# Layer-2 attention scores as 64-row products in both row halves of the array

## The chip, the cores and the metric

The kernel runs on one core of one Trainium2 chip. The metric is the device time of one execution in microseconds (us). The engines are TensorE (PE, whose weight loads are listed apart as PEld), VectorE (DVE), ScalarE (ACT), GpSimd (POOL) and SyncE (SP, which issues most of the DMAs). Each engine works through its own instructions in a fixed order and waits for the others at semaphores.

## The reference, cut to what matters

The program is a Mamba block (layer 0) and then a position-attention block (layer 1 in the reference's count, the "second layer" here) on x of shape (4, 512, 32, 32). Only the second layer is touched by the change:

```python
x_top    = conv1x1(x, w_top,    b_top)     # (b, 64, 1024): 64 channels, hw = 1024
x_center = conv1x1(x, w_center, b_center)  # (b, 64, 1024)
x_bottom = conv3x3(x, w_bottom, b_bottom)  # (b, 512, 1024)
sp_map = einsum('bnp,bpm->bnm', x_center.T, x_top)      # p = 64: the scores, 1024 x 1024
sp_map = softmax(sp_map.reshape(b, -1), axis=1)         # over all of an image's scores at once
sp_map = einsum('bnm,bmc->bnc', sp_map, x_bottom.T)
out = conv3x3(x + sp_map.reshape(b, c, h, w), w_out, b_out)
```

The sum over p in the scores has 64 terms, half of the 128 rows of the PE array. The softmax is over a whole image, so nothing may be exponentiated before the maximum of all 1024 x 1024 scores of that image is known.

## The kernel before, in words

Layer 0 is one long planned stream and ends at about 1866 us of the profiled span. The second layer follows, image by image (b = 0 to 3), and there the order of each engine's instructions is set by the tile framework's scheduler: it moves instructions of one engine past each other where data allow it, and what it chose is then fixed.

For each image the work goes through these functions.

- `norm` (for images 1 to 3) normalises the image into the padded tile `xg`.
- `scores` computes `pt`, the top and center convolutions at once: four accumulating 128x512 products for each half h of the pixels, top channels in partitions 0 to 63 of `pt`, center channels in 64 to 127. ACT copies them to SBUF with the bias, `center` in one 64x512 instruction and `top` in four 64x128 ones, since top's columns are reordered into four row phases r and two column phases k. Both tiles hold 128 partitions: the data sit in 0 to 63, and two POOL memsets write zeros into 64 to 127. Then for each of eight blocks m of 128 top columns and each half h, one product `psc` (128 rows, half of them zeros) goes to a PSUM bank, ACT copies the bank to `st[m]`, and after both halves DVE takes the row maximum into `mx`.
- After the eighth block DVE reduces `mx` to `mp`, POOL takes the maximum over partitions (`partition_all_reduce`, tile `ma`), DVE negates it, and ACT exponentiates the eight `st` tiles with the sums into `rs`, which DVE reduces to `rp`.
- `conv3` computes the 3x3 convolution by a Winograd scheme. POOL and DVE make the row inputs `rr` (from `e`, `f`, then `g`, `h`, then `k`, `l`, in a ring of four buffers), DVE `spread`s them into `v` (four instructions, lines 1461 to 1464), and PE makes 24 products `m`, each of four accumulating 128x512 matmuls with a 1 MB weight tile `uw` that SP loads into a ring of three. The products go by pairs of row points, (1,2), (3,4), (0,5), and for each point p through q = 2, 1, 0, 3. `m[2]` is read by ACT into `e_b` (line 1588), `m[1]`, `m[0]` and `m[3]` by DVE into `n_b` (line 1596).
- `attend` multiplies the exponentiated scores with the convolution (`pat`) and adds the result to `xg`; then `conv3` runs again with the output weights (`m_o`), and `turn_back` transposes its result (`po`) and adds it to `o`.

PSUM has eight banks here: pool `pm` with a ring of five for the `m` products, and pool `ps` with a ring of three for everything else (`pt`, `psc`, `pat`, `po`). A new tile can be written only when the tile that held its bank before has been read. So product (2,1) of a convolution needs the bank of (1,2), which is free after ACT's `e_b` of point 1, and (3,1) needs the bank of (2,2), free after `e_b` of point 2.

The convolution of image b and the scores of image b are independent up to `attend`, and PE runs `psc` and the first `m_b` products close together. ACT's instructions in the order before: copies of `psc`, `e_b` of point 1, the eight exponentials, `e_b` of point 2. For images 1 and 3 ACT and POOL also prepare the output convolution of the image before (`e_o`, `f_o`, then POOL's `g_o`, `h_o`) in the same stretch; the order on POOL there is `e_o`, `g_o`, `ma`, `f_o`, `h_o`.

The tiles `top` and `center` come from pool `fp`, tag `f4`, a ring of three that they share with the output tiles `o` of `finish`. For image 2 this matters: `o_3` of image 1 takes the buffer of `o_0`, `top` that of `o_1` and `center` that of `o_2`, each once its store has landed.

Of the kernel before, what the change touches and what calls it, by code (L numbers as in the profile page):

```python
# [8 lines left out]
F32 = mybir.dt.float32  # L9
AF = mybir.ActivationFunctionType  # L10
ALU = mybir.AluOpType
AX = mybir.AxisListType
# [3 lines left out]
P = 128  # L16
B, C, HH, WW = 4, 512, 32, 32
L = HH * WW
# [5 lines left out]
T = 512  # L24
NH = L // T
NB = B * NH
PAB = 64
# [4 lines left out]
    xp=(1, 2, 1),  # L32
# [184 lines left out]
def mamba_then_pab_kernel(  # L217
# [25 lines left out]
    nc = tc.nc  # L243
# [20 lines left out]
    pb_sb = cpool.tile([P, 1], F32, tag="pb", name="pb_sb")  # L264
# [58 lines left out]
    with ExitStack() as l0:  # L323
# [985 lines left out]
        for b in range(B):  # L1309
            at = b * NDC * NS  # L1310
            for n in range(NDC):
                e, h = divmod(n, NH)
# [30 lines left out]
    with ExitStack() as l1:  # L1343

        pm = l1.enter_context(tc.tile_pool(name="l1pm", bufs=5, space=PSUM))
        ps = l1.enter_context(tc.tile_pool(name="l1ps", bufs=3, space=PSUM))
        wp = l1.enter_context(tc.tile_pool(name="l1w", bufs=1))

        TI, TJ = HH // 4, WW // 2
# [6 lines left out]
        xp = l1.enter_context(tc.tile_pool(name="l1x", bufs=2))  # L1356
        fp = l1.enter_context(tc.tile_pool(name="l1f", bufs=3))

        NMC = L // P
# [40 lines left out]
        def scores(b, xg):  # L1400

            top = fp.tile([P, L], F32, tag="f4", name=f"top_{b}")
            center = fp.tile([P, L], F32, tag="f4", name=f"center_{b}")
            nc.gpsimd.memset(top[PAB:P, :], 0.0)
            nc.gpsimd.memset(center[PAB:P, :], 0.0)
            for h in range(NH):
                pt = ps.tile([P, T], F32, tag="ps", name=f"pt_{b}_{h}")
                for c in range(NCC):  # L1410
                    nc.tensor.matmul(
                        pt, wt_sb[:, c].rearrange("p j n -> p (j n)"),
                        xg[:, c, 1 + h * HR : 1 + (h + 1) * HR, 1 : WW + 1],
                        start=(c == 0), stop=(c == NCC - 1),
                    )
                nc.scalar.activation(
                    center[0:PAB, h * T : (h + 1) * T], pt[PAB:P], AF.Identity, bias=pb_sb[PAB:P]
                )
                tv = top[0:PAB].rearrange("p (r k i j) -> p r i j k", r=4, k=2, j=TJ)
                pv = pt[0:PAB].rearrange("p (i r j k) -> p r i j k", r=4, j=TJ, k=2)  # L1420
                hi = slice(h * TI // 2, (h + 1) * TI // 2)
                for r in range(4):
                    nc.scalar.activation(
                        tv[:, r, hi], pv[:, r], AF.Identity, bias=pb_sb[0:PAB]
                    )
            mx = spool.tile([P, NMC], F32, tag="mx", name=f"mx_{b}")
            st = []
            for m in range(NMC):
                t = xp.tile([P, L], F32, tag="st", name=f"st_{b}_{m}", bufs=NMC)
                for h in range(NH):  # L1430
                    pt = ps.tile([P, T], F32, tag="ps", name=f"psc_{b}_{m}_{h}")
                    nc.tensor.matmul(
                        pt, top[:, m * P : (m + 1) * P], center[:, h * T : (h + 1) * T],
                        start=True, stop=True,
                    )
                    nc.scalar.copy(t[:, h * T : (h + 1) * T], pt)
                nc.vector.reduce_max(mx[:, m : m + 1], t, axis=AX.X)
                st.append(t)
            mp = spool.tile([P, 1], F32, tag="mp", name=f"mp_{b}")
            nc.vector.reduce_max(mp, mx, axis=AX.X)  # L1440
            ma = spool.tile([P, 1], F32, tag="ma", name=f"ma_{b}")
            nc.gpsimd.partition_all_reduce(ma, mp, P, bass_isa.ReduceOp.max)
            nc.vector.tensor_scalar_mul(ma, ma, -1.0)
            rs = spool.tile([P, NMC], F32, tag="rs", name=f"rs_{b}")
            for m in range(NMC):
                nc.scalar.activation(
                    st[m], st[m], AF.Exp, bias=ma, accum_out=rs[:, m : m + 1]
                )
            rp = spool.tile([P, 1], F32, tag="rp", name=f"rp_{b}")
            nc.vector.reduce_sum(rp, rs, axis=AX.X)  # L1450
            return st, rp
# [251 lines left out]
        left = list(range(EARLY, NPC))  # L1703
        half = len(left) // 2
        st, rp = scores(0, image[0])
        for a in range(0, B, 2):
            ins = None
            for b in (a, a + 1):
                xb = conv3(f"b{b}", image[b], ub, brow[0], behind=ins)
                also = left[b * half : (b + 1) * half] if not a else []  # L1710
                after, v = iter(()), None
                if b == a:
                    after = norm(b + 1)
                    next(after)
                    next(after)
                else:
                    v = first_inputs(f"o{a}", image[a])
                ins = attend(b, image[b], st, rp, xb, after, also)
                if b == a:
                    st, rp = scores(b + 1, image[b + 1])  # L1720
            if a + 2 < B:
                after = norm(a + 2, True)
                next(after)
            y = conv3(f"o{a}", image[a], uo, brow[1], v)
            next(after, None)
            finish(a, y)
            if a + 2 == B:
                last(a + 1, image[a + 1], None)
                break
            next(after, None)  # L1730
            finish(a + 1, conv3(f"o{a + 1}", image[a + 1], uo, brow[1]))
            st, rp = scores(a + 2, image[a + 2])
# [57 lines left out]
```

## Time and profile before

| what | value |
|---|---|
| median of 3 runs | 2896.76 us (2893.47, 2896.76, 2897.07) |
| profiled execution, its own time | 2893.83 us |
| its span | 2892.0 us |
| mean granted TensorE clock over the span | 0.988 |
| DVE busy over the span | 2284.7 us (79%) |
| ACT busy over the span | 1837.3 us (64%) |
| POOL busy over the span | 2041.5 us (71%) |
| `psc`: PE busy, 128 instructions (64 products of two passes each) | 55.8 us |
| `st<-psc` copies on ACT, 64 of 586 ns median | 37.5 us |
| `mx` reductions on DVE, 32 of 1214 ns median | 38.2 us |
| `top`, `center` memsets on POOL, 8 of 0.95 us median | about 8 us |

A product of fp32 data shows in the trace as two weight loads and two matmul passes. The listed duration of a pass (592 ns for 512 columns) is its latency; passes follow each other every 0.43 us, so that 32 passes, the scores of one image, last 13.97 us. A timeline row gives the start, the length from the first start to the last end, the engine, the line, the operation, the tile written and the tiles read, how many instructions are merged, and in brackets how long the engine stood idle before and what it waited for. The "idle" of PEld between two loads has no weight: loads run ahead of the matmuls.

### The profile page before, as it was taken

The page shows a single profiled execution, that of the slowest core. Times are in us where ns is not written, and L with a number is a line of the kernel's source. Part 1 is how long each engine was busy: PE and PEld are TensorE (multiplying, and loading weights), DVE is VectorE, ACT ScalarE, POOL GpSimd, SP SyncE. Part 2 cuts the span into 40 slices and gives each one's busy share as a digit, 9 for nine tenths or more (in the row PEclk, how much of TensorE's full clock was granted, in tenths as well). Part 3 has the DMA queues.
Part 4 walks back from the last instruction along what each step waited for, and adds up shares of the span by engine and source line. Part 5 has one row for each costly group of instructions (what it writes and reads, how often), then busy time and mean ns, then how long its engine had stood idle before and what let it go on. Part 6 is the DMA issues. An engine that isn't in the chain of part 4 may idle for free.

```text
span 2892.0 us, 36189 instructions
## 1 busy us (share of the span) xinstructions
PE 2712.5 (94%) x11720; PEld 1614.8 (56%) x11720; DVE 2284.7 (79%) x2724; ACT 1837.3 (64%) x3249; POOL 2041.5 (71%) x1243
## 2 busy tenths in 40 slices
PE   6898799999999999989989999799999999999998
PEld 2455566666676566666667766544444444444444
DVE  5579999989999889989899999868776655356254
ACT  4789899999899999899999999530300003030000
POOL 6899999899998999999999999733231341223222
PEclk9999999999999999999999999999999999999999
DMA  6766655577655577645565664768789886436587
GB/s 188 204 178 196 185 165 176 160 216 243 196 170 168 163 230 227 200 145 176 161 206 175 212 195 144 186 225 259 255 275 300 317 321 241 180 138 226 174 313 261
DMA packets 406260, 603.68 MB, mean 209 GB/s; under 512 B 47192, under 2 KB 246104, under 8 KB 381496
## 3 DMA queue, kind: packets, MB, share of 16 engines
q1 hardware_dynamic: 398456, 587.11, 64.0%
q10 hardware_dynamic: 7616, 14.26, 1.4%
q8 instruction: 94, 1.54, 0.2%
q14 instruction: 94, 0.77, 0.1%
HBM read 504.27 MB, written 96.99 MB: 208 GB/s over the span
## 4 chain that ended last, share of the span: by engine, by line
PE 44%; ACT 21%; DVE 14%; POOL 9%; issue 7%; DMA 5%; SPq 0%; POOLq 0%; DVEq 0%; ACTq 0%
PE m_o L1580 11%; PE m_b L1580 8%; ACT sc L917 5%; PE y L990 4%; DVE da L957 4%; PE pat L1632 4%; ACT da L904 4%; POOL da L980 4%; PE u L943 4%; PE po L444 3%; ACT u L904 3%; PE pxm L444 2%; PE pz L444 2%; ACT L251 2%; POOL dbx L932 1%
## 5 line engine op out<-in xcount | busy, mean ns | idle before, releaser
L980 POOL TENSOR_TENSOR da<-da,cbc 128x1024 f32<-128x1024 f32 x314 | 742.3, 2370 | 33.0 <-DVE da L957 8.3
L917 ACT ACTIVATE sc<-dtxt,bt_sb 128x256 f32<-128x256 f32 x1256 | 550.6, 498 | 18.1 <-PE u L943 17.4
L932 POOL TENSOR_TENSOR dbx<-dtx,bbc 128x1024 f32<-128x1024 f32 x198 | 467.5, 2371 | 20.3 <-PE y L990 8.8
L904 ACT ACTIVATE da<-dt,a_sb 128x512 f32<-128x512 f32 x628 | 433.5, 714 | 13.6 <-PE y L990 8.8
L957 DVE TENSOR_TENSOR_SCAN da<-da,u 128x512 f32<-128x512 f32 x328 | 383.0, 1203 | 39.7 <-PE u L943 23.0
L943 PE MATMUL u<-ident,sc 128*128 128x128 f32 x2512 | 362.3, 278 | 32.8 <-DVE da L957 19.0
L943 PEld LDWEIGHTS u<-ident,sc 128*128 128x128 f32 x2512 | 291.8, 142 | 160.5 <-issue 48.5
L957 DVE TENSOR_TENSOR_SCAN da<-da,carry_sb,u 128x512 f32<-128x512 f32 x300 | 367.3, 1261 | 14.3 <-PE u L943 10.9
L990 PE MATMUL y<-ident,da 128*128 128x128 f32 x2512 | 338.4, 276 | 29.3 <-POOL da L980 28.5
L1580 PE MATMUL m_o<-uw_o,v_o 128*128 128x512 f32 x768 | 335.7, 596 | 7.4 <-DMA uw_o<-u_o 7.4
L990 PEld LDWEIGHTS y<-ident,da 128*128 128x128 f32 x2512 | 288.7, 142 | 93.7 <-POOL da L980 54.7
L1580 PE MATMUL m_b<-uw_b,v_b 128*128 128x512 f32 x768 | 333.8, 593 | 6.2 <-ACT e_b L1588 2.9
L904 ACT ACTIVATE u<-dt,a_sb 128x512 f32<-128x512 f32 x396 | 262.4, 680 | 10.9 <-DVE da L957 6.4
L444 PE MATMUL pxm<-xt,winc 128*128 128x345 f32 (+3 forms) x704 | 243.0, 488 | 19.0 <-DVE xs L706 4.7
L1580 PEld LDWEIGHTS m_b<-uw_b,v_b 128*128 128x128 f32 x768 | 144.8, 190 | 191.6 <-issue 180.3
L1580 PEld LDWEIGHTS m_o<-uw_o,v_o 128*128 128x128 f32 x768 | 144.9, 191 | 189.8 <-issue 178.4
L444 PE MATMUL pz<-xt,winc 128*128 128x512 f32 x512 | 239.5, 599 | 1.4 <-ACT dtxt L881 1.0
L990 PE MATMUL y<-ident,dbx 128*128 128x128 f32 x1584 | 220.0, 276 | 12.7 <-DVE dbx L973 7.1
L980 POOL TENSOR_TENSOR dbx<-dbx,cbc 128x1024 f32<-128x1024 f32 x91 | 215.4, 2367 | 15.2 <-DVE dbx L957 6.9
L1632 PE MATMUL pat<-y_b,st 128*128 128x512 f32 x512 | 221.6, 593 | 1.5 <-DVE rz L1641 1.4
L990 PEld LDWEIGHTS y<-ident,dbx 128*128 128x128 f32 x1584 | 182.6, 141 | 49.3 <-issue 22.7
L1588 ACT ACTIVATE e_o<-m_o 128x512 f32<-128x512 f32 x24 | 14.3, 597 | 276.2 <-PE m_o L1580 261.8
(226 smaller groups left out, 4242.2 us busy)
## 6 DMA issues: line engine op xcount, KB each, us to landing
cbc<-bcd SPq DMA_DIRECT2D x512, 256.0 KB, 3.6
uw_b<-u_b SPq DMA_DIRECT2D x96, 1024.0 KB, 4.8
uw_o<-u_o SPq DMA_DIRECT2D x96, 1024.0 KB, 4.8
bbc<-bcd SPq DMA_DIRECT2D x198, 256.0 KB, 4.0
u_b<-work SPq DMA_DIRECT2D x192, 128.0 KB, 2.6
winc<-in_w_in_dram SPq DMA_DIRECT2D x72, 256.0 KB, 3.7
szd<-sz SPq DMA_DIRECT2D x32, 512.0 KB, 4.3
szl<-szd SPq DMA_DIRECT2D x32, 512.0 KB, 5.1
```

Source lines behind the costliest of these rows:

```text
L251: nc.scalar.preload_act_table_set("natural_log_exp_and_others")
L444: lambda k=k, lhs=lhs, rhs=rhs: nc.tensor.matmul(p()[:, at : at + cols], lhs(), rhs(), start=(k == 0), stop=(k == n - 1)),
L904: nc.scalar.activation(t, dt()[:, j], AF.Exp, scale=a_sb[:, at : at + 1])
L917: nc.scalar.activation(sc()[:, k], dtxt()[:, k], AF.Copy, scale=bt[:, at, s : s + 1])
L932: lambda: nc.gpsimd.tensor_mul(hc(), dtx(), b_bc().to_broadcast([P, 2, T])),
L943: nc.tensor.transpose(u()[:, k * P : (k + 1) * P], sc()[:, k, j, :], ident)
L957: nc.vector.tensor_tensor_scan(ht, *((hc()[:, j], u()) if on_act else (u(), hc()[:, j])), carry_sb[:, j, s : s + 1] if h else 0.0, ALU.mul ...
L980: nc.gpsimd.tensor_mul(hc(), hc(), c_bc().to_broadcast([P, 2, T]))
L990: nc.tensor.matmul(y[j]()[:, k, :], hc()[:, j, k * P : (k + 1) * P], ident, start=(s == 0 and k == 0), stop=(s == NS - 1 and k == NK - 1), ...
L1580: nc.tensor.matmul(m[q], v[:, q, k, c, :], w[:, c, :], start=(c == 0), stop=(c == NCC - 1 and not extra),)
L1588: nc.scalar.activation(e, m[2], AF.Copy, scale=al / 2)
L1632: nc.tensor.matmul(pt, st[m][:, 2 * P * j + h : 2 * P * (j + 1) : 2], xb[m // 2][:, m % 2, :], start=(m == 0), stop=(m == NMC - 1),)
```

## The change

The score products contract over 64 rows instead of 128. `top` and `center` no longer have zero rows: partitions 0 to 63 and 64 to 127 both hold data. `center` is written twice, to the lower half by ACT as before and to the upper half by DVE (`tensor_scalar_add`, straight from the same PSUM partitions). `top` is split by column phase k: even blocks m = 2r lie in partitions 0 to 63 and odd ones in 64 to 127, so ACT writes it in two instructions of 64x256 for each half where there were four of 64x128. The eight memsets are gone. The eight blocks are taken by pairs: for each half h, the even block's product is issued from the lower 64 rows into a bank of pool `ps`, then the odd block's from the upper 64 rows into a bank of pool `pm`. The copies to `st` and the maxima are as many as before, in pairs.

```diff
             center = fp.tile([P, L], F32, tag="f4", name=f"center_{b}")
-            nc.gpsimd.memset(top[PAB:P, :], 0.0)
-            nc.gpsimd.memset(center[PAB:P, :], 0.0)
             for h in range(NH):
...
                 nc.scalar.activation(
                     center[0:PAB, h * T : (h + 1) * T], pt[PAB:P], AF.Identity, bias=pb_sb[PAB:P]
                 )
-                tv = top[0:PAB].rearrange("p (r k i j) -> p r i j k", r=4, k=2, j=TJ)
-                pv = pt[0:PAB].rearrange("p (i r j k) -> p r i j k", r=4, j=TJ, k=2)
+                nc.vector.tensor_scalar_add(
+                    center[PAB:P, h * T : (h + 1) * T], pt[PAB:P], pb_sb[PAB:P]
+                )
+                pv = pt[0:PAB].rearrange("p (i r j k) -> p k r i j", r=4, j=TJ, k=2)
                 hi = slice(h * TI // 2, (h + 1) * TI // 2)
-                for r in range(4):
+                for k in range(2):
+                    tv = top[k * PAB : (k + 1) * PAB].rearrange(
+                        "p (r k i j) -> p k r i j", r=4, k=2, j=TJ
+                    )
                     nc.scalar.activation(
-                        tv[:, r, hi], pv[:, r], AF.Identity, bias=pb_sb[0:PAB]
+                        tv[:, k, :, hi], pv[:, k], AF.Identity, bias=pb_sb[0:PAB]
                     )
...
-            for m in range(NMC):
-                t = xp.tile([P, L], F32, tag="st", name=f"st_{b}_{m}", bufs=NMC)
+            for g in range(0, NMC, 2):
+                two = [
+                    xp.tile([P, L], F32, tag="st", name=f"st_{b}_{g + k}", bufs=NMC) for k in range(2)
+                ]
                 for h in range(NH):
-                    pt = ps.tile([P, T], F32, tag="ps", name=f"psc_{b}_{m}_{h}")
-                    nc.tensor.matmul(
-                        pt, top[:, m * P : (m + 1) * P], center[:, h * T : (h + 1) * T],
-                        start=True, stop=True,
-                    )
-                    nc.scalar.copy(t[:, h * T : (h + 1) * T], pt)
-                nc.vector.reduce_max(mx[:, m : m + 1], t, axis=AX.X)
-                st.append(t)
+                    pts = [
+                        pool.tile([P, T], F32, tag=tag, name=f"psc_{b}_{g}_{h}_{tag}")
+                        for pool, tag in ((ps, "ps"), (pm, "m"))
+                    ]
+                    for k, pt in enumerate(pts):
+                        rows = slice(k * PAB, (k + 1) * PAB)
+                        nc.tensor.matmul(
+                            pt, top[rows, (g + k) * P : (g + k + 1) * P],
+                            center[rows, h * T : (h + 1) * T], start=True, stop=True,
+                        )
+                    for t, pt in zip(two, pts):
+                        nc.scalar.copy(t[:, h * T : (h + 1) * T], pt)
+                for k, t in enumerate(two):
+                    nc.vector.reduce_max(mx[:, g + k : g + k + 1], t, axis=AX.X)
+                st.extend(two)
```

The built program of the changed kernel gives the order that the scheduler now chooses in the second layer; layer 0 has the same order as before. What moves:

- DVE, image 0: the upper `center` of half 0 comes before the two `rr_b` of pair (1,2), that of half 1 after them and before the four `v_b`. In the `n_b` of point 1, `rp` moves ahead of the last one.
- DVE, images 1 and 3: the upper `center` of half 0 comes after the first of the four `v_b` (1461), that of half 1 after all four. `rr_b`, `v_b` and `mx` follow, interleaved slightly differently; `mp` comes again after the second `rr_b` of pair (0,5).
- DVE, image 2: `o_3`, then the upper `center` of half 0, two `rr_b`, the upper `center` of half 1, the maxima. All `n_b` of point 1 now stand behind `rp`, and ACT's `e_b` of point 1 behind the exponentials.
- POOL, images 1 and 3: `e_o`, `f_o`, `g_o`, then `ma`; before, `f_o` stood behind `ma`.
- PE: all 16 `psc` follow `pt` directly and stand ahead of the first `m_b`. Before, two matmuls of (1,2) stood ahead of them for images 1 and 3, and all of (1,2) and (1,1) for image 2. The first product of the upper half in each half h of the pixels waits for DVE.
- SP, image 2: the load of `o_3` comes before the fourth weight load instead of after it.

## The prediction

> **What bounds the kernel now.** I read the page's busy rows first, then the groups of PE from 1860 us on (the second layer), then the waits and the timelines around the scores of each image. The busy rows and three PE groups:
>
> ```profile
> span 2892.0 us, 36189 instructions
> PE 2712.5 (94%) x11720; PEld 1614.8 (56%) x11720; DVE 2284.7 (79%) x2724; ACT 1837.3 (64%) x3249; POOL 2041.5 (71%) x1243
> ...
> L1580 PE MATMUL m_b<-uw_b,v_b 128*128 128x512 f32 x768 | 333.8, 593 | 6.2 <-ACT e_b L1588 2.9 <-DVE y_b L1620 1.6 <-DMA uw_b<-u_b 0.9
> ...
> L1432 PE MATMUL psc<-center,top 128*128 128x512 f32 x128 | 55.8, 593 | 1.3 <-POOL f_b L1481 1.3
> ```
>
> PE hardly rests in the second layer, so a microsecond of PE time there is a microsecond of the end unless another chain takes over. The m_b row names such a chain: PE already waits 2.9 us for ACT's e_b. The scores are 4 x 13.97 us of PE. Their surroundings decide what a saving is worth, so I take the images one by one. Image 1, by engine (PE, DVE, POOL, ACT in turn):
>
> ```profile
> 2047.14 13.90 PE L1432 MATMUL psc<-center,top 128*128 128x512 f32 x32
> 2067.16 24.30 PE L1580 MATMUL m_b<-uw_b,v_b 128*128 128x512 f32 x56
> 2093.56 32.02 PE L1580 MATMUL m_b<-uw_b,v_b 128*128 128x512 f32 x74 [2.10 <-ACT e_b L1588]
> ...
> 2044.04 1.23 DVE L1461 TENSOR_TENSOR v_b<-rr_b 128x1024 f32<-128x1024 f32 x1
> 2045.18 3.56 DVE L1462 TENSOR_TENSOR v_b<-rr_b 128x1024 f32<-128x1024 f32 x1
> 2048.66 3.58 DVE L1463 TENSOR_TENSOR v_b<-rr_b 128x1024 f32<-128x1024 f32 x1
> 2052.15 1.25 DVE L1464 TENSOR_TENSOR v_b<-rr_b 128x1024 f32<-128x1024 f32 x1
> ...
> 2070.97 3.27 POOL L1481 TENSOR_TENSOR e_o<-e_o,xg 128x1088 f32<-128x1088 f32 x1 [19.83 <-ACT e_o L1480]
> 2074.21 2.52 POOL L1543 TENSOR_TENSOR g_o<-xg 128x1088 f32<-128x1088 f32 x1
> 2083.20 0.38 POOL L1442 PARTITION_ALL_REDUCE ma<-mp  x1 [6.48 <-issue]
> 2090.80 2.29 POOL L1481 TENSOR_TENSOR f_o<-f_o,xg 128x1088 f32<-128x1088 f32 x1 [7.22 <-ACT st L1446]
> ...
> 2092.93 1.05 ACT L1588 ACTIVATE e_b<-m_b 128x512 f32<-128x512 f32 x2
> ```
>
> The end of this stretch is not set by PE: POOL does e_o and g_o, then spends 6.48 us before the reduction, ACT exponentiates, and only then reads the bank that PE's product (3,1) needs. PE stands 2.10 us, and 0.85 us at the same place in image 3 (a wait ending at 2600.81). DVE has no hole from 2040 to 2074.
>
> **The products.** Sixteen products take 13.97/16 = 0.87 us each. No row has two products in different row halves, so the price of a pair lies between one product (0.87) and two (1.74). I take 0.87: the two passes of a product use other rows than those of the next. ACT's two e_b above show its rate, 1.05 us for two or about 0.5 a copy; 16 copies need some 8 us and fall little behind. So 16 products would take 7 us, if nothing stands in between. [...]
>
> **What stands in between: DVE's upper center.** The first odd product of half 1 needs DVE's second copy, and PE's order lets nothing pass it. No row shows a 64x512 copy from PSUM on DVE; the nearest is n_b (128x512, one PSUM operand), 0.68 us alone and 0.60 in a row. Bounds 0.3 (half the elements) to 0.7; I take 0.6.
>
> *Image 0.* The two rr_b in front of it run 1881.04 to 1885.85, so the copy ends at about 1886.5, while PE would have had its first pair done by 1882.9. From 1886.6 on, seven slots of 0.87 remain: PE leaves the scores at 1892.7, where before it left at 1895.2. PE has stood 3.7 us by then, and what follows a stand shows in the stretches just before (columns: PE, PEld, DVE, ACT, POOL busy, then the granted clock):
>
> ```profile
> 1867.00:1871.00 4.00, 1.20 (x6) 0.59 (x4) 2.88 (x10) 0.47 (x2) 3.25 (x7) 1.00 0.78 205
> 1871.00:1873.40 2.40, 2.39 (x3) 0.80 (x4) 2.40 (x3) 0.00 (x0) 0.84 (x1) 0.59 1.04 423
> 1873.40:1876.00 2.60, 2.60 (x6) 1.17 (x5) 0.44 (x1) 2.08 (x2) 2.03 (x1) 0.72 1.00 422
> ```
>
> After 4 us with 1.2 of work the clock was 0.59, then 0.72: 2.4 x 0.41 + 2.6 x 0.28 = 1.7 us lost. So PE leaves at 1892.7 to 1894.4. [...]
>
> Then banks: product (2,0), at 1916.9 before, needs the bank of (1,1), read by DVE's n_b. DVE before: mp 1904.37, ma 1909.24. After, one more v_b (1.15) and one copy (0.6) stand ahead: mp 1906.1, ma 1911.0; then a v_b, two rr_b (1.2 each) and the n_b pair (1.28), until 1915.9. So (2,0) starts at 1916.1: a gain of 0.8, whatever PE saved. Bounds: -2.5 (DVE as early as before) to +2.5 (two v_b of 3.5 us, as in image 1). Value -0.8.
>
> *Image 1.* The second copy follows all four v_b: 2053.4 plus two copies, 2054.6. PE stands from 2048 on. Seven slots then end at 2060.8 (2062.5 at the lower clock), and product (1,2), of which two matmuls came first before, has 4 x 0.86 to do instead of 1.72. PE reaches (3,1) at 2091.5 + 1.7 + 0 to 1.6, 2093.2 to 2094.8. But e_b: its chain through POOL has f_o in front of ma now. e_o starts as before (rr_b has four v_b and six mx ahead, where it had seven, plus two copies: -1.14 + 1.2), and f_o adds 2.3 (the row at 2090.80) to 3.3 (the e_o row, with DVE busy). I take 2.3 and 0.1: ma and e_b 2.4 late, PE resumes at 2096.0. Loss 2.4, bounds 0 (f_o hidden) to 3.4.
>
> *Image 3.* Same order of instructions, and PE arrives earlier than e_b here too: DVE's second copy is at 2560.5, seven slots 2566.6, against 2569.4 before with two matmuls ahead. Loss 2.4, same bounds.
>
> *Image 2.* Before, PE filled its waits with all of (1,2), (1,1) and the bias, and the scores ran 2399.98 to 2413.91. Now nothing fills them. pt of half 1 needs a bank that o_3's additions free. o_3's load waits for the store of o_0, issued at 2385.25; the memset of top, waiting for o_1's store, ran at 2389.50. Its load, issued at about 2388.7 and no longer behind 1 MB of weights, takes the 2.6 (least) to 4.5 us (median) to land that the view of tile o gives: 2391.3 to 2393.2. Additions 1.4, pt 3.45, ACT's center and top about 1.6: the first pair at 2398.8, eight slots to 2405.8, then (1,2), (1,1), bias (3.44 + 3.44 + 1.05): 2413.7, where before it was 2413.9. Half of a clock loss of 1.7 on top and 0.5 for rounding: +1.2, bounds -3 to +3. DVE's n_b of point 1 and ACT's e_b move behind the exponentials; maxima end 5 us earlier at 2410.7, POOL's 6.26 us ahead of ma is then past, e_b comes at 2421 and (2,1) only at 2424: no wait.
>
> The eight memsets (0.95 us each) cost nothing before: POOL stood idle beside them (8.70, 12.49 us). The ACT top copies get shorter by 0.3 us, hidden in the wait for DVE. The row switch: the one-row bias matmul pushes the next load from 0.43 to 0.95 us; two switches an image, about 1 us, fall into the stands for images 0, 1 and 3.
>
> **Sum.** -0.8 + 2.4 + 1.2 + 2.4 = +5.2 us. Against the profiled execution, 2893.83 us (2892.0 of span), 2899.0. It lies 2.93 below the median of the runs, 2896.76; by the median 2902.0.
>
> **The rivals.**
> - *Serial.* The two halves do not overlap. 13 products after the stand take 11.3 instead of 6.1 us: image 0 +3.4, image 1 +5.5 (PE now later than e_b), image 2 +7.4, image 3 +3.3 (2571.8 against 2567.7, less the 0.85 wait): +19.6, 2916.4. For it: no row shows overlap. Against it: the bank and row of each pair are distinct. Chance 0.20.
> - *Gain.* DVE's second copy of half 1 is there in time, in images 0 and 2, before the first pair is done; decides from 1883 in image 0. Then 7 us come through twice, and images 1 and 3 still lose 2.4: -9.2, 2887.6. Against it: rr_b of 3.61 us in front of the copy, and the n_b bank at 1916. Chance 0.11.
> - *Nothing.* f_o hides in the 6.48 us in front of ma, so that ma is not late: -0.8 + 0.1 + 1.2 + 0.1, 2897.4. Against it: that time follows g_o's end in image 1 and a memset's end in image 2 (6.26), so it looks like work of POOL itself. Chance 0.13.
>
> **How the numbers follow.** The forecast, 2902.0, has chance 0.56; its own range from the bounds is 2896 to 2908. 0.2% of the median is 5.8 us, about what a measurement of this kernel tells from no change. The forecast splits 0.27 slower, 0.28 same, 0.01 faster; serial is slower; the gain is 0.10 faster, 0.01 same; nothing is 0.11 same, 0.01 slower, 0.01 faster. Together faster 0.12, same 0.40, slower 0.48. The range runs from halfway to the gain (2891) to the serial case (2916).
>
> **What would show it.** Right: an idle row before psc naming DVE center, 3 to 7 us in images 0, 1 and 3; psc of 6 to 8 us after it; the clock below 1 there; POOL's order e_o, f_o, g_o, ma with ma 2.4 later relative to e_o; PE's wait for e_b grown in images 1 and 3. Wrong: psc passes 0.43 apart after the stand (serial), no stand (gain), ma at its old distance (nothing), or any new idle of PE that I don't name.

## The result and the profile after

| | before | after |
|---|---|---|
| median of 5 runs each, on one chip | 2896.76 us | 2907.72 us |
| profiled execution, its own time | 2893.83 us | 2907.88 us |
| its span | 2892.0 us | 2906.1 us |
| from the first `pt` pass of image 0 to the end of the span | 1021.0 us | 1034.5 us |

The ratio after to before is 1.0047 with a 95% interval of [1.0034, 1.0060] (the two medians alone, 11.0 us apart, give 1.0038): the change made the kernel slower by 10 to 17 us. One execution of e6 below, the profiled one, and one of e7 ran at a mean granted clock of 0.749 and took 3515 and 3518 us; the ratios leave them out, and no profile of e6 is used. The last row leaves out the first layer, which the change does not touch; its end differs by 0.6 us between these two executions and by up to 4.5 us between all the profiled executions used below, so stages are compared from there on.

The head of the page after:

```profile
span 2906.1 us, 36162 instructions
...
PE 2702.1 (93%) x11720; PEld 1621.5 (56%) x11720; DVE 2293.1 (79%) x2732; ACT 1830.8 (63%) x3233; POOL 2029.6 (70%) x1235
```

PE is busy 10.4 us less than before (2712.5) and the span is 14.1 us longer: some 24 us of new idle time. The list of PE's waits in the second layer after (wait, total, times, longest) says where most of it is:

```profile
PE psc_ps L1442 <- ACT top L1426: 25.5, 4, 9.9
PE m_o L1592 <- DMA uw_o<-u_o: 6.0, 4, 5.1
PE m_b L1592 <- DMA uw_b<-u_b: 3.3, 2, 2.0
PE pt L1409 <- DVE o L1690: 2.9, 1, 2.9
```

Before, PE waited 1.3 us ahead of the scores, once. Now it waits four times, and for ACT's `top`, not for DVE's `center`. The timeline after around the scores of image 0 shows why (start, length, engine, line, operation, tile written and read, count, idle before and releaser):

```profile
1877.08 0.69 ACT L1414 ACTIVATE center<-pt,pb_sb 64x512 f32<-64x512 f32 x1 [1.13 <-PE pt L1409]
1877.87 0.76 DVE L1417 TENSOR_SCALAR center<-pt,pb_sb 64x512 f32<-64x512 f32 x1 [4.11 <-ACT center L1414]
1878.66 0.95 ACT L1426 ACTIVATE top<-pt,pb_sb 64x256 f32<-64x256 f32 x2 [0.90 <-DVE center L1417]
1880.53 0.69 ACT L1414 ACTIVATE center<-pt,pb_sb 64x512 f32<-64x512 f32 x1 [0.92 <-PE pt L1409]
1880.90 3.61 DVE L1495 TENSOR_TENSOR rr_b<-e_b,f_b 128x1088 f32<-128x1088 f32 x1 [2.27 <-POOL f_b L1493]
1884.43 1.28 DVE L1496 TENSOR_TENSOR rr_b<-e_b,f_b 128x1088 f32<-128x1088 f32 x1
1885.74 0.76 DVE L1417 TENSOR_SCALAR center<-pt,pb_sb 64x512 f32<-64x512 f32 x1
...
1886.53 0.96 ACT L1426 ACTIVATE top<-pt,pb_sb 64x256 f32<-64x256 f32 x2 [5.32 <-DVE center L1417]
1887.06 1.22 PE L1442 MATMUL psc_ps<-center,top 64*128 64x512 f32 x1 [6.56 <-ACT top L1426]
1887.55 1.22 PE L1442 MATMUL psc_m<-center,top 64*128 64x512 f32 x1
1888.07 1.06 PE L1442 MATMUL psc_ps<-center,top 64*128 64x512 f32 x1
...
1893.06 0.59 PE L1442 MATMUL psc_ps<-center,top 64*128 64x512 f32 x1
...
1893.31 0.59 PE L1442 MATMUL psc_m<-center,top 64*128 64x512 f32 x1
1893.48 0.59 PE L1442 MATMUL psc_ps<-center,top 64*128 64x512 f32 x1
```

All three copies only read the bank `pt`, but in every image they run one after another in program order: ACT's center, DVE's upper center, ACT's top (ACT idles 0.90 to 4.03 us ahead of `top` for DVE's first copy and 0.82 to 6.41 us for its second). DVE's second copy stands behind two `rr_b`; ACT idles 5.32 us for it, and PE 6.56 us for ACT. `top` is the weight of every product, so already the first pair waits.

The last three rows show that the overlap itself works: a pass into `psc_ps` and one into `psc_m` start within 0.42 us (1893.06 to 1893.48), where before one pass took 0.43 us. But that is the pace only from 1893 on. The windows after of the same stretch (columns: PE, PEld, DVE, ACT, POOL busy, granted clock, DMA share, GB/s):

```profile
1881.00:1887.00 6.00, 0.00 (x0) 0.00 (x0) 5.94 (x4) 0.68 (x2) 3.50 (x2) 0.64 0.00 1
1887.00:1893.00 6.00, 5.94 (x14) 4.82 (x16) 6.00 (x3) 3.05 (x7) 4.85 (x2) 0.51 0.01 3
1893.00:1897.20 4.20, 4.20 (x21) 3.00 (x17) 4.20 (x4) 4.18 (x10) 0.00 (x0) 1.00 0.00 0
```

For 6 us after the stand the clock is half (0.51): the scores last 10.3 us (1887.06 to 1897.33) where e4 below, at a granted clock of 1.00, needs 7.6. They last 10.5, 9.3 and 9.5 us in images 1 to 3.

### The profile page after: what moved, and what is told of

Read it like the earlier page. It is cut to its first block, busy times and chain, and to the rows that moved or that the text cites. A ratio compares the mean times of both kernels' runs of the same rounds, so it can differ in the third digit from the quotient of the medians.

```text
span 2906.1 us, 36162 instructions
## 1 busy us (share of the span) xinstructions
PE 2702.1 (93%) x11720; PEld 1621.5 (56%) x11720; DVE 2293.1 (79%) x2732; ACT 1830.8 (63%) x3233; POOL 2029.6 (70%) x1235
## 4 chain that ended last, share of the span: by engine, by line
PE 47%; ACT 20%; DVE 14%; POOL 8%; DMA 5%; issue 5%; SPq 1%; DVEq 0%; POOLq 0%; ACTq 0%
PE m_o L1592 11%; PE m_b L1592 11%; ACT sc L917 5%; DVE da L957 4%; PE y L990 4%; PE pat L1644 4%; ACT da L904 4%; POOL da L980 4%; PE u L943 3%; PE pxm L444 3%; PE po L444 3%; ACT u L904 3%; PE pz L444 2%; DVE u L957 2%; ACT L251 2%
## 5 line engine op out<-in xcount | busy, mean ns | idle before, releaser
L957 DVE TENSOR_TENSOR_SCAN da<-da,carry_sb,u 128x512 f32<-128x512 f32 x300 | 367.3, 1261 | 13.7 <-PE u L943 10.3
L1600 ACT ACTIVATE e_o<-m_o 128x512 f32<-128x512 f32 x24 | 14.3, 598 | 275.7 <-PE m_o L1592 261.3
## 6 DMA issues: line engine op xcount, KB each, us to landing
uw_b<-u_b SPq DMA_DIRECT2D x96, 1024.0 KB, 4.8
uw_o<-u_o SPq DMA_DIRECT2D x96, 1024.0 KB, 4.8
```

The costliest lines, as they stand in the source:

```text
L957: nc.vector.tensor_tensor_scan(ht, *((hc()[:, j], u()) if on_act else (u(), hc()[:, j])), carry_sb[:, j, s : s + 1] if h else 0.0, ALU.mul ...
L1600: nc.scalar.activation(e, m[2], AF.Copy, scale=al / 2)
```

## The experiments

Three theories, each a part of the change: **A**, `top` waits behind DVE's upper copy, so PE stands (6.56 us in image 0) and then runs at half clock (0.51); **C**, POOL does `f_o` too ahead of the maximum (before, only `e_o` and `g_o`), which makes `e_b` late in images 1 and 3; **D**, the bank from the pool of `m` lets no product of the convolution run ahead of the scores. **B** is the rival that alternating row halves itself costs time. All ratios are to the kernel before on the same chip, with 95% intervals; 0.001 is 2.9 us. The median of the kernel before differs between the sessions (2896.76 us with the change; 2892.06, 2893.47, 2894.62 and 2895.00 with the experiments), so an expectation given in us fits only roughly, and the ratio decides. "C undone" goes one step further than the kernel before: `e_o` goes behind the maximum as well as `f_o`.

| run | what differs | ratio |
|---|---|---|
| after | | 1.0047 [1.0034, 1.0060] |
| e1_act_upper | A undone | 1.0041 [1.0028, 1.0054] |
| e13_after_max_first | C undone | 1.0031 [1.0019, 1.0043] |
| e6_max_first | A and C undone | 1.0008 [0.9998, 1.0017] |
| e7_one_pool | D undone | 1.0020 [1.0009, 1.0030] |
| e14_three_undone | A, C and D undone | 0.9975 [0.9961, 0.9989] |
| e2_dve_last | DVE's copy behind top | 1.0002 [0.9993, 1.0011] |
| e9_dve_last_one_pool | the same, D undone | 1.0003 [0.9993, 1.0012] |
| e3_lower_only | before, 64 rows in one half | 1.0006 [0.9996, 1.0017] |
| e4_act_late_exp | A undone, late exponentials | 1.0003 [0.9993, 1.0014] |
| e5_before_late_exp | before, late exponentials | 0.9990 [0.9981, 0.9998] |
| e11_late_max_first | A, C undone, late exponentials | 0.9995 [0.9984, 1.0006] |
| e12_all | A, C, D undone, late exponentials | 0.9980 [0.9968, 0.9992] |

**e1_act_upper: A alone.**

```diff
-                nc.vector.tensor_scalar_add(
-                    center[PAB:P, h * T : (h + 1) * T], pt[PAB:P], pb_sb[PAB:P]
-                )
+                nc.scalar.activation(
+                    center[PAB:P, h * T : (h + 1) * T], pt[PAB:P], AF.Identity, bias=pb_sb[PAB:P]
+                )
```

> The changed kernel with the upper center copy on ScalarE instead of VectorE; nothing else differs. Theory A (the loss comes from ScalarE's top copies, which wait for VectorE's upper center copy of the same bank, so that even the first pair of products stands behind v_b and rr_b): the stands of 6.6, 9.9 and 7.0 us ahead of the products of images 0, 1 and 3 shrink to under 2 us, the products take 7 to 8 us in place of 9.2 to 10.4, the clock stays near 1 there. The order on POOL is unchanged, so in images 1 and 3 TensorE then comes before e_b and waits for it about 2 to 5 us; image 2 gains 2 to 5 us. Total 2895 to 2901, a ratio to before of 0.999 to 1.0015. Theory B (the alternation of row halves is itself the cost: a lower clock or a switch at each pass): the products still take 9 to 10 us each, total 2904 to 2908. Theory C (POOL's f_o ahead of the maximum sets the end in images 1 and 3): no more than image 0 and 2 come back, ma stays 14.5 us behind e_o, total 2899 to 2903.

2902.8 us, 1.0041: far above A's range, and by the ratio above what C expected too (2903 us is 1.0022 of 2896.76). The stands did shrink, to 1.95 us in every image, and yet hardly any time came back. PE's waits in e1 show what took their place:

```profile
PE m_b L1592 <- ACT e_b L1600: 9.0, 2, 5.3
PE psc_ps L1442 <- ACT top L1426: 7.8, 4, 2.0
...
PE m_b L1592 <- DVE n_b L1608: 5.3, 2, 3.3
```

Of 25.5 us of stands, 17.7 went, and 14.3 us of waits for `e_b` and `n_b` came. So A alone is not the loss. Even in image 0, where C has no part, the gain did not last: e1 came to product (2,0) 43.8 us after `pt` and the change 47.5, but from `pt` of image 0 to `pt` of image 1 both took the same (168.9 and 168.7). Against B, the products of image 0 took 7.6 us at a granted clock of 1.00. In the other three they took 9.1 to 9.3, although the stand was the same 1.95 us.

**e13_after_max_first: C alone.** `e_o` and `f_o` of the next convolution are queued on POOL behind the reduction.

```diff
-            nc.gpsimd.partition_all_reduce(ma, mp, P, bass_isa.ReduceOp.max)
+            peak[b] = nc.gpsimd.partition_all_reduce(ma, mp, P, bass_isa.ReduceOp.max)
...
-                    v = first_inputs(f"o{a}", image[a])
+                    with tc.issue_after(peak[b].ins):
+                        v = first_inputs(f"o{a}", image[a])
```

> The changed kernel with POOL's e_o and f_o put behind the maximum over the partitions; the upper copy stays on VectorE ahead of top, two pools as in the change. In the changed kernel TensorE did not wait for e_b, since it came 2 us later than e_b by itself. Theory A+C (two chains of nearly the same length: TensorE behind top's wait, and e_b behind the maximum; taking one away alone brings nothing): 2903 to 2908, ratio 1.003 to 1.006. Rival (the order on POOL alone is the loss, through n_b and the banks too): 2896 to 2901.

1.0031, at the lower edge of what A+C expected; the intervals of e13 and of the change overlap. In images 1 and 3 nothing changed for PE: from `pt` to the convolution's product (1,0) it took 35.25 and 32.37 us, against 35.50 and 31.61 after. Of the 4.7 us that the profiled execution won from `pt` of image 0 to the end (1029.8 against 1034.5), 2.3 lie in image 2 (29.06 us from `pt` against 31.35), where `pt` of half 1 was not slowed (3.68 us against 5.37). That is not what theory C is about.

**e6_max_first: A and C together** (the two diffs above).

> The first run's kernel (upper copy on ScalarE) with POOL's e_o and f_o of the next convolution put behind the maximum over the partitions; g_o stays in front. In the first run the stand was gone and 9.0 us of new waits for e_b and 5.3 us for n_b had come up. Theory C (the order on POOL, the maximum behind e_o and f_o, is what gives the saved time back in images 1 and 3): the maximum comes some 5.6 us earlier there, TensorE's waits for e_b fall from 9.0 us to under 2, total 2889 to 2896, about 9 us below the first run. Rival: the 6.5 to 7.8 us that POOL spends in front of the reduction follows g_o's end whatever is in front, and DVE's part (mx, mp) is late too, so the waits stay above 5 us: 2898 to 2903.

1.0008 (2896.6 us), at the upper end of what C expected (2896), and 0.0033 or 9.5 us below e1, where C had about 9. Taken away alone, A brings 0.0006 and C 0.0016; together 0.0039, some 11 us. Each of these ratios is uncertain by about 0.0013 either way, so the joint gain is clear of the noise, neither single one is, and that the joint gain is more than their sum (by 0.0017) is not shown by the ratios. It is what two chains of almost equal length would give, and the traces show such chains: in images 1 and 3 after, PE came to product (3,1) at 2099.9 and 2616.3 (2075.80 and 2592.19 plus 56 passes of 0.43), and `e_b` was done at 2098.1 and 2616.0. For image 1:

```profile
2075.80 75.80 PE L1592 MATMUL m_b<-uw_b,v_b 128*128 128x512 f32 x176
2097.55 0.58 ACT L1600 ACTIVATE e_b<-m_b 128x512 f32<-128x512 f32 x1
```

Where e6 itself waits is not known.

**e7_one_pool: D alone.**

```diff
-                        pool.tile([P, T], F32, tag=tag, name=f"psc_{b}_{g}_{h}_{tag}")
-                        for pool, tag in ((ps, "ps"), (pm, "m"))
+                        pool.tile([P, T], F32, tag=tag, name=f"psc_{b}_{g}_{h}_{k}")
+                        for pool, tag, k in ((ps, "ps", 0), (ps, "ps", 1))
```

> The changed kernel with the banks of both products of a pair from the pool of three that the scores had before, and none from the pool of the convolution; the upper copy stays on VectorE ahead of top. TensorE then takes products of the running convolution ahead of the scores again (two of four matmuls of (1,2) in images 1 and 3, some in image 2), as in the kernel before. Theory A: the stand in images 0, 1 and 3 stays at about 6.6, 9 and 6 us because top still waits for VectorE; only image 2 gets its filling back, 3 to 5 us of the 4.7 lost there; total 2901 to 2906. Rival D (the second pool, which lets nothing of the convolution pass the scores, is the main loss): 2893 to 2899. With three banks for 16 products ScalarE's copies of 0.48 us may pace the products: 7.7 to 9 us in an image.

1.0020, some 8 us below the change although 15.6 us of stands behind `top` are still there: in us (2898.3) it falls into D's range, by the ratio (2902.6 on the scale of 2896.76) into A's, so both are partly met. PE in image 2 of e7:

```profile
2392.94 3.61 PE L1409 MATMUL pt<-xg,wt_sb 128*128 128x512 f32 x8
2396.38 3.59 PE L1592 MATMUL m_b<-uw_b,v_b 128*128 128x512 f32 x8
2399.92 3.71 PE L1409 MATMUL pt<-xg,wt_sb 128*128 128x512 f32 x8
2403.56 1.12 PE L1597 MATMUL m_b<-brow_b,ones 1*128 1x512 f32 x2
2404.61 1.98 PE L1592 MATMUL m_b<-uw_b,v_b 128*128 128x512 f32 x4
2406.52 10.11 PE L1442 MATMUL psc<-center,top 64*128 64x512 f32 x32
```

After the change PE stood in these places (2.90 us ahead of `pt`, 2.07 ahead of the scores) and then ran at a lower clock (0.67 to 0.71 in `pt` of half 1, 0.56 in the first 3.9 us of the scores); here products of the convolution fill them and there is no stand. Counted from the first `po` of the turn-back to product (1,0), image 2 takes 29.2 us (with four passes that were done earlier), against 37.2 after and 32.5 before. These 8 us are as much as the ratio says that e7 won; its profiled execution won 10.5 from `pt` of image 0 on (1024.0 against 1034.5), the rest of it behind these places, while image 0 lost 1.6. With three banks the products of this image take 10.1 us in place of e4's 7.6: each bank has to be copied out by ACT before it comes round (in e14's image 0, where they take the same 10.1 us, PE's weight loads wait 0.19 to 0.65 us at a time for ACT's `st`).

**e14_three_undone: A, C and D together** (the three diffs above; exponentials as in the change).

> The changed kernel with its three suspected faults taken away and nothing else: the upper copy on ScalarE (no wait behind VectorE), both banks from the pool of three (the convolution fills the waits again), e_o and f_o behind the maximum. The exponentials are where the changed kernel has them. The run before it, which has late exponentials as well, came to 0.998 of the kernel before, and late exponentials alone to 0.999. If the halves bring something of their own once the three are gone: 2888 to 2892, ratio 0.998 to 0.9995. If they bring nothing and the late exponentials were all of it: 2893 to 2897.

0.9975, better than expected and faster than both kernels. The products take 10.1 us in all four images, at a granted clock of 1.00 where it was read (images 0 and 1), and there is no stand ahead of them in images 1 and 2. PE from `pt` of image 1 to product (3,1) in e14:

```profile
2034.51 7.15 PE L1411 MATMUL pt<-xg,wt_sb 128*128 128x512 f32 x16
2042.59 1.96 PE L1594 MATMUL m_b<-uw_b,v_b 128*128 128x512 f32 x4 [0.94 <-DMA uw_b<-u_b]
2044.48 10.11 PE L1444 MATMUL psc<-center,top 64*128 64x512 f32 x32
2054.52 5.42 PE L1594 MATMUL m_b<-uw_b,v_b 128*128 128x512 f32 x12
2059.87 1.12 PE L1599 MATMUL m_b<-brow_b,ones 1*128 1x512 f32 x2
...
2089.49 54.62 PE L1594 MATMUL m_b<-uw_b,v_b 128*128 128x512 f32 x120 [4.28 <-ACT e_b L1602]
```

Of the waits that the change touches, the one that is left is for `e_b`, 6.3 us in all (4.3 in image 1): the saved time is not yet through there. How much of the 7 us against the kernel before comes from the halves is open, since e14 also puts `e_o` behind the maximum, and no run gives the kernel before that order. Its waits for `e_b`, which such an order could shorten, were 2.9 us, and e5 below, where they are gone, gained 0.0010 of e14's 0.0025.

**e2_dve_last and e9_dve_last_one_pool.** The wiring that the prediction assumed: DVE's copy is written behind the two `top` copies, so that ACT does not wait for it. e9 adds the diff of e7.

```diff
-                nc.vector.tensor_scalar_add(
-                    center[PAB:P, h * T : (h + 1) * T], pt[PAB:P], pb_sb[PAB:P]
-                )
                 pv = pt[0:PAB].rearrange("p (i r j k) -> p k r i j", r=4, j=TJ, k=2)
...
+                nc.vector.tensor_scalar_add(
+                    center[PAB:P, h * T : (h + 1) * T], pt[PAB:P], pb_sb[PAB:P]
+                )
```

> The changed kernel with the upper center copy still on VectorE, but written behind the two top copies, so that it reads the bank last and ScalarE does not wait for it. This is the wiring that the prediction assumed. Theory A: the even products of half 0 start at once and TensorE stands at the first odd product instead (half 0's second copy is late by the same VectorE work), so the stand is cut by the first pass only; about 3.7 us in image 0 as the prediction had it; total 2900 to 2906. If the stand keeps its length although ScalarE no longer waits, the queue on VectorE alone sets it and the bank order cost nothing: 2906 to 2909. Theory B: 2904 to 2908 with products at 9 to 10 us.

> Both edits: the upper copy behind top on VectorE (second run) and one pool of three banks. The second run came to 2892.4, with 11.0 us of stands behind VectorE's copy and lost filling in image 2. Theory A with D: stands behind VectorE stay near 8 to 11 us in images 0, 1 and 3 because only two matmuls fill them; image 2 gets back 3 to 5 us: 2887 to 2891. If the two edits do not add, 2892 or more.

e2 came to 1.0002, by the ratio some 3 us better than theory A allowed (2900 us is 1.0011 of 2896.76). The edit also turned POOL's order round, which the expectation left out. POOL in image 1 of e2:

```profile
2067.53 1.43 POOL L1454 PARTITION_ALL_REDUCE ma<-mp  x1 [19.33 <-DVE mp L1452]
2076.02 2.31 POOL L1493 TENSOR_TENSOR e_o<-e_o,xg 128x1088 f32<-128x1088 f32 x1 [7.06 <-ACT st L1458]
```

The maximum comes first and PE never waits for `e_b`, so the time by which the stands are shorter can come through; that this is the whole reason is not shown. As the prediction said for this wiring, PE's stand is now at an odd product: 2.83, 4.92 (two stands) and 3.24 us in images 0, 1 and 3, naming DVE's `center`. So e2 undoes C and part of A; it is no test of A alone. e9 won nothing over e2 (1.0003), so D undone is worth 0.0027 beside the change and 0.0033 beside e6, but nothing beside e2. In the profiled executions e9 wins 5.9 us in image 2 (161.9 against 167.8 from the first `po` of the turn-back to `pt` of image 3) and loses 5.3 in image 0 (172.8 against 167.5 from `pt` to `pt` of image 1). There the products from three banks take 15.7 us with the stand in them, against 14.0 in e2; the rest of the loss is not traced.

**e3_lower_only: the rows alone.** The kernel before, without zero rows and without alternation.

```diff
-            nc.gpsimd.memset(top[PAB:P, :], 0.0)
-            nc.gpsimd.memset(center[PAB:P, :], 0.0)
...
-                        pt, top[:, m * P : (m + 1) * P], center[:, h * T : (h + 1) * T],
+                        pt, top[0:PAB, m * P : (m + 1) * P], center[0:PAB, h * T : (h + 1) * T],
```

> The kernel before with its products over the lower 64 rows alone: no zero rows, no memsets, no second copy, no alternation. Theory A: products of 64 rows that follow each other in the same half cost what products of 128 cost (0.87 us each, 13.9 us in an image), VectorE is not in the chain, total 2893 to 2899, as before. Theory B (the row mode or its switch costs time or clock by itself): products longer than 13.9 us or new idle ahead of them and behind them, total 2900 or more. If the eight memsets cost something before, total under 2892.

1.0006, no difference to be seen. The scores take 14.00 us in each image, against 13.90 to 14.00 before: here a product of 64 rows costs what one of 128 costs, and only the pair in different halves saves (7.6 us an image in e4). No cost of the memsets is to be seen. With e4's 7.6 us and e14's 10.1 in all four images there is no sign of B.

**e4, e5, e11, e12: late exponentials.** The eight exponentials and their sum are written behind the call of the third convolution.

```diff
+            return st, ma
+
+        def weights(b, st, ma):
+
             rs = spool.tile([P, NMC], F32, tag="rs", name=f"rs_{b}")
...
                 xb = conv3(f"b{b}", image[b], ub, brow[0], behind=ins)
+                rp = weights(b, st, ma)
```

e4 is e1 with it, e5 the kernel before with it, e11 is e6 with it, e12 is e14 with it.

> The kernel of the first run (upper copy on ScalarE) with the eight exponentials and their sum written behind the call of the third convolution, so that e_b and n_b of the running convolution come ahead of them in the queues. Theory A with C: what is left of the loss in images 1 and 3 is the chain POOL maximum, exponentials, e_b; with e_b free of it TensorE's wait for e_b there goes to under 0.5 us, and the saved products come through: 2882 to 2893, ratio 0.995 to 0.9985. Theory B: no more than 2 us below the first run.

> The kernel before with the eight exponentials and their sum written behind the call of the third convolution, and nothing else; the scores stay products of 128 rows. This tells how much of the fourth run's time is the late exponentials and how much the halves. Before, TensorE waited 2.1 and 0.85 us for e_b: at best these 2.9 us come through, 2889 to 2892; if the exponentials are then late for the attention products behind them, 2892 to 2896.

> Upper copy on ScalarE, exponentials written late, e_o and f_o behind the maximum, two pools. The fourth run (without the last edit) had 4.2 us of waits for e_b and 6.0 for n_b, at 2892.6. If theory C holds the waits for e_b go and those for n_b shrink to the 3.2 us of image 0; each stand taken away also takes away the lower clock behind it: 2884 to 2889, ratio 0.997 to 0.999. If something else takes the place of these waits: 2891 to 2894.

> As the run before it, with the banks of both products from the pool of three. The products then take about 10.1 us (three banks) in place of 7.6, but products of the convolution fill the wait ahead of them in images 1, 2 and 3. Theory A+C+D: in images 1 to 3 about 3.8 us of TensorE time come through in each, less what the waits for the banks of n_b take: 2878 to 2886, ratio 0.995 to 0.998, the fastest of all. If the late exponentials alone are the gain, as in the kernel before with them (0.999): 2888 to 2892.

e5 met its forecast: 0.9990, PE's 2.9 us for `e_b` are gone. e4 came to 1.0003 and missed its range (0.995 to 0.9985), though it is 0.0038 below e1, far more than B allowed. The waits for `e_b` fell only from 9.0 to 4.2 us: in images 1 and 3 the scheduler put `e_b` of point 2 behind six of the eight exponentials instead of all eight, and the first of them still waits for the maximum. Its products took 7.6 us in all four images (granted clock 1.00 in images 0 to 2, not read in image 3), in image 0 7.62 us, from the start of the first to the end of the last of these rows:

```profile
1880.33 0.69 PE L1442 MATMUL psc_ps<-center,top 64*128 64x512 f32 x1 [1.95 <-ACT top L1426]
...
1886.93 1.02 PE L1442 MATMUL psc_m<-center,top 64*128 64x512 f32 x2
```

How much of e4's gain is the clock and how much the earlier `e_b` is not separated. e11 missed (0.9995): 5.7 us of waits for `n_b` and 3.3 for `e_b` stayed. e12 reached 0.9980, at the upper end of its range of ratios; beside e14's 0.9975 no gain of late exponentials is to be seen once A, C and D are undone. The waits for `e_b` went down from 6.3 to 0.4 us there, but those for `n_b` went up from 0.7 to 7.2.

## Why the prediction was right, and where not

It forecast 2902.0 us, slower, and 2907.72 is inside its range, just under the upper end (2908) that its own bounds give; of the 11 us between the medians it found 5. Of its signs, the clock below 1 and POOL's new order came; the stand came but named `top`, the products took 9.3 to 10.5 us instead of 6 to 8, and PE's wait for `e_b` did not grow but went. By terms, from `pt` of each image to the same product of the convolution (image 0: (2,0); images 1 and 3: (3,1); image 2: from the first `po` to (1,0)):

| term | forecast | measured |
|---|---|---|
| image 0 | -0.8 | +1.7 (47.5 us against 45.8) |
| image 1 | +2.4 | +3.5 (59.6 against 56.1) |
| image 2 | +1.2 | +4.7 (37.2 against 32.5) |
| image 3 | +2.4 | +1.9 (55.7 against 53.8) |

The sum is +11.8 of the 13.5. Of the rest, the waits for `uw_b` are 2.4 us longer (3.3 against 0.9) and those for `uw_o` 1.4 shorter (6.0 against 7.4).

- **The overlap** was right (0.43 us a pair of passes); the serial rival fell.
- **The step that failed** is "The first odd product of half 1 needs DVE's second copy, and PE's order lets nothing pass it." It was the first product of all, since ACT's `top` waits for DVE's copy of the same bank. The stand was 6.56 us in image 0 for 3.7, and 9.89 and 6.98 us in images 1 and 3. DVE's place behind `rr_b` and `v_b` was read rightly; the copy itself took 0.76 us, outside the bounds of 0.3 to 0.7. Why the framework orders these reads is not shown: `top` reads partitions 0 to 63 of the bank and DVE's copy 64 to 127, and ACT still waits 5.32 us.
- **The clock** was mis-sized: at most 1.7 us for a stand; the scores lost 2.7, 2.9, 1.7 and 1.9 us to it (10.3, 10.5, 9.3, 9.5 less e4's 7.6; granted 0.51, 0.50 and 0.56 behind the stands of images 0 to 2, not read in image 3), and `pt` of half 1 in image 2 another 1.7 (5.37 against 3.68; granted 0.67 to 0.71).
- **Image 0's bank**, DVE's `n_b`, was not decisive after, because PE came later still. e1 shows it as the next limit: with the stand gone PE waits 3.34 us for `n_b` and resumes 43.8 us after `pt`, where the prediction had 45.1 and before had 45.8.
- **The chain through POOL** was sized rightly and not the one that decided. In image 1 after:

```profile
2073.24 2.29 POOL L1493 TENSOR_TENSOR e_o<-e_o,xg 128x1088 f32<-128x1088 f32 x1 [19.56 <-ACT e_o L1492]
2075.50 3.34 POOL L1493 TENSOR_TENSOR f_o<-f_o,xg 128x1088 f32<-128x1088 f32 x1
2078.80 2.52 POOL L1555 TENSOR_TENSOR g_o<-xg 128x1088 f32<-128x1088 f32 x1
2087.82 0.38 POOL L1454 PARTITION_ALL_REDUCE ma<-mp  x1 [6.50 <-issue]
```

  From `e_o` to `ma` it is 14.58 us, 2.35 more than before (12.23), as forecast. But PE came 1.8 us later than `e_b` by itself (2099.9 against 2098.1), so the wait for `e_b` that the prediction named as the sign of being right is not there. e1 brings it back (9.0 us), and e6 shows that both have to go. That images 1 and 3 came out near the forecast, 3.5 and 1.9 us for 2.4 each, is luck: the loss came by PE's stand and clock, and the chain that was costed happened to be as long.
- **Image 2** had the right order of events and too small a price: that nothing fills the waits any more was seen, but it was costed on a full clock for `pt` and half a loss for the scores. e4's image 2, at a granted clock of 1.00 and without DVE in the chain, takes 33.3 us from the first `po`, +0.8: near the forecast. e7 shows that the filling is worth 8 us there. A reading was off too, without weight: the scores before started at 2399.91, not 2399.98, and halfway from the forecast to the gain is 2894.8, not 2891.

A loss can be larger than the waits: in e1 the 120 passes behind the wait of 3.72 us for `e_b` last 54.54 us, in e14 behind one of 4.28 us 54.62, in e7 behind one of 1.00 us 51.77. That the clock is the reason is the author's estimate; it was not read over these rows.

What stays open: why the same stand is followed by half clock in some images and not in others (below), whether e13's 0.0016 is more than that, why one pool brings nothing beside e2, and how much the halves are worth by themselves in e14.

## What to carry to other kernels

When a second engine is given a copy out of a PSUM bank, look at every later reader of that bank: here `top` waited for the new copy's place in DVE's queue (ACT idled 5.32 us in image 0, 6.41 in image 1), so the copy belongs behind the readers on the critical path or on their engine, and the order on every other engine has to be read again after the edit (e2). A second pool for a stage's banks also decides what may run ahead of that stage, and the filling lost can be worth more than the faster stage (8 us in image 2 of e7, against the 2.5 us between products of 10.1 and 7.6). When taking a suspected wait away brings next to nothing (0.0006 in e1, 0.0016 in e13), look for a second chain of the same length and take both away (0.0039 in e6) before the theory is dropped.

## What the runs showed of the hardware

**The clock after a short stand is not a function of the stand's length alone.** Two kernels, the same place, the same stand of 1.95 us in image 1. The windows of e1 (the figure after the five engines is the granted clock):

```profile
2043.60:2045.50 1.90, 0.00 (x1) 0.00 (x0) 1.90 (x2) 1.84 (x3) 1.90 (x1) 1.00 1.16 349
2045.50:2050.00 4.50, 4.45 (x13) 3.39 (x15) 4.50 (x2) 2.38 (x6) 4.26 (x2) 0.62 0.87 303
```

The same view of e4:

```profile
2043.10:2045.00 1.90, 0.01 (x1) 0.00 (x0) 1.90 (x2) 1.83 (x3) 1.90 (x1) 1.00 1.09 335
2045.00:2049.50 4.50, 4.44 (x20) 2.63 (x22) 4.50 (x2) 3.75 (x9) 4.50 (x2) 1.00 0.93 316
```

Ahead of the stand PE was busy without a gap at a granted 1.00 in both, from 2028.00 to 2043.60 in e1 and to 2043.00 in e4; behind it passes into `psc_ps` follow each other every 0.85 us in e1 (2046.48 to 2049.04) and every 0.43 us in e4. Three of e1's four score stages ran partly at half clock, images 1 and 2 at a granted 0.62 and 0.57 and image 3 with passes 0.85 us apart; none of e4's did (7.6 us each). What decides between them is not shown: no run here shifted a stand on purpose.

**POOL spent 6 to 8 us between a tensor operation and the reduction, and 7 to 9 behind it.** Ahead of `ma` in image 1 it was 6.48 us before, 6.50 after, 7.76 in e1 and 6.03 in e13 with `g_o` in front, and 8.11 in e7 with `f_o` in front. Behind it the next tensor operation, `h_o`, came 7.70 us later after and 9.00 in e1, with no wait that the profile shows. Where POOL had been idle for 19.33 us (e2) the reduction began 0.14 us after the end of `mp` (2067.39). What POOL does in these 6 to 8 us is not shown.

**A small copy on DVE was not cheap:** 0.76 us for 64x512 from PSUM, more than the 0.68 of a single 128x512 `n_b`.
